# Four conditional layers on one core: first loads in another order, both sines of a rotation together, and the last three queries copied out and normed later

## The chip, the cores and the metric

The kernel runs on 1 core of one Trainium2 chip. Times are device microseconds of that core. TensorE (PE) multiplies, VectorE (DVE), ScalarE (ACT) and GpSimd (POOL) work on elements, SyncE (SP) issues most DMAs; ACT and POOL issue some too.

## The reference

64 sequences of 64 tokens with 512 features pass four residual layers; small integer tables choose per sequence which weights are used.

```python
x = x + (einsum('bsi,bio->bso', x, W0[id]) + b0[id][:, None, :])          # L0, 16 experts
x = x + (einsum('btd,od->bto', x, W1) + s[a] * (x @ A[a].T) @ Bm[a].T)    # L1, 8 adapters of rank 16
# L2: paged attention, 8 query and 4 key heads of 64, window 256, pos = kv_len + 0..63
q, k, v = x @ Wq.T, x @ Wk.T, x @ Wv.T
q, k = rope(rms(q, q_norm_scale), pos), rope(rms(k, k_norm_scale), pos)
# k, v are written into the paged blocks, then attention over the last 256 positions
x = x + softmax(mask(q @ k_all.T / 16)) @ v_all @ Wo.T
x = x + (einsum('bct,bcd->bdt', x, W3[subject]) + bias[subject][:, :, None])   # L3
```

Here `rms(x, g)` is `x * rsqrt(mean(x*x) + 1e-6) * (1 + g)`, and `rope` turns each half-pair by the angle `pos * inv`, with its sine and cosine. All is float32.

## The kernel before

The 4096 tokens are 32 tiles of 128 rows (two sequences each). Every engine runs its instructions in the order in which the program writes them (`manual_schedule`), and so do the queues: the order of the calls is the schedule.

**Phase one** (to about 520 us) goes through the tiles in groups of 1, 1, 2 and then 4. `layer0(i)` multiplies a tile by its two experts' matrices, which `load_w0` fetched (2 x 1 MB a tile, buffers for two tiles); ACT copies the product out as s0; `add_bias` (POOL) makes x plus the bias; `turn0` transposes s0 on PE and DVE adds the two. `layer1(tiles)` multiplies a group by w1 (to whose diagonal blocks the identity is added, for the residual) and by the adapters: pxa, xa, then bo on top. `turn_x2` transposes the result; `keep_kv` makes, norms and rotates the keys and stores them with the values; `parts_q` does that for the queries of earlier tiles and `turn_q` transposes a finished query and stores it to qTd.

`turned` is the common norm and rotation: ACT squares, DVE reduces, ACT takes the square root, then after a `yield` DVE's reciprocal and product, after another `yield` two half products with the sine, one with the cosine (DVE) and an add (engine `X`). `rotation(o)` makes sine and cosine for eight tiles in DVE steps separated by `yield`s, each ending with a Sin on ACT; `other(i)` advances it, `windows` (the row indices of the attention window) and the copies of old cache rows between two matmul groups.

**First loads.** SP loads the tokens' tables (tok1), x of tile 0, W0 of tile 0 in four pieces for one expert (ACT's queue takes the other's), w1, two adapters, x and W0 of tile 1, and so on. Ahead of its W0 pieces ACT's queue issues idcol, toki (all tables to 128 partitions), invf and gain. The bias rows are gathered by POOL (brow), transposed on PE behind the first `layer0` and copied to biasT by ACT (L673).

**The passage.** `gains` for the last seven tiles are made ahead. POOL gathers the keys and values of attention tiles 0 and 1 (`load_kv`), PE makes the queries of tiles 25 to 30 (`product`, L140), which go through `parts_q` on DVE, with `turn_q` (L174) two tiles behind. Then `keys(0)` transposes keys (L823, L829).

**Phase two**: step s of 32 issues `load_kv(s+2)` on POOL and the mask loads on SP, then `scores(s)` (PE L842; DVE adds the mask and takes the maximum, L850; ACT takes the exponential, L854), `attend(s-1)` (L889), `normalise(s)` (DVE), on even steps `last(s-4)` (L929, ACT L936), `project(s-2)` (L917, into the one bank of the pool `pyp`), `keys(s+1)` and `turn(s)` (transposes L875 and L879, copied out by DVE and ACT, L876 and L880). Everything else on PSUM shares a ring of seven banks. The query of tile 31 is made in step 0, in the bank of `pyp`; those of 30 and 31 are rotated and turned in steps 1 to 5:

```python
        else:
            parts[NT - 1] = parts_q(NT - 1, product(NT - 1, wq, "pq", pyp), V, cs[NT - 1])
            turn_q(NT - 3, bp)
        if s == 2:
            next(parts[NT - 1])
        normalise(s, 0)
```

Of the kernel before, what the change touches and what calls it, by code (L numbers as in the profile page):

```python
# [59 lines left out]
def body(ctx: ExitStack, tc: tile.TileContext, a: dict, out: bass.AP):  # L60
# [54 lines left out]

    def turned(ps, n, to, pool, X, kind, cg, sg):

        psv = ps[:, : n * HD].rearrange("p (h d) -> p h d", d=HD)
        sq = pool.tile([128, n, HD], F32, name=f"sq{kind}", bufs=2)
        S.activation(sq, psv, AF.Square)  # L120
        ss = pool.tile([128, n], F32, name=f"ss{kind}", bufs=2)
        V.tensor_reduce(ss, sq, AX.X, ALU.add)
        S.activation(ss, ss, AF.Sqrt, bias=epst, scale=1.0 / HD)
        yield
        rs = pool.tile([128, n], F32, name=f"rs{kind}")
        V.reciprocal(rs, ss)
        qn = pool.tile([128, n, HD], F32, name=f"qn{kind}", bufs=2)
        V.tensor_tensor(qn, psv, bc(rs[:, :, None], [128, n, HD]), ALU.mult)  # L128
        yield
        t2 = sq  # L130
        for f in range(2):
            fs, of = slice(f * HALF, (f + 1) * HALF), slice((1 - f) * HALF, (2 - f) * HALF)
            V.tensor_tensor(t2[:, :, fs], qn[:, :, of], bc(sg[:, None, fs], [128, n, HALF]), ALU.mult)
        V.tensor_tensor(qn, qn, bc(cg[:, None, :], [128, n, HD]), ALU.mult)  # L134
        X.tensor_tensor(to, qn, t2, ALU.add)  # L135
# [6 lines left out]

    def parts_q(i, pq, X, cs=None):
        qr = late.tile([128, H, HD], F32, name="qr", bufs=2)
        qrs[i] = qr.rearrange("p h d -> p (h d)")
        return turned(pq, H, qr, late, X, 0, *(cs or gains(0, i, late, X)))

# [22 lines left out]
    def turn_q(i, pool=late):  # L170
        qrf = qrs.pop(i)
        pqt = bank("pqt")
        for c in range(KC):
            TE.transpose(pqt[:, c * 128 : (c + 1) * 128], qrf[:, c * 128 : (c + 1) * 128], ident)  # L174
        qT = pool.tile([128, 2, 2, 2, T], F32, name="qTs", bufs=2 if pool is late else 4)
        for gp in range(2):
            S.copy(
                qT[:, gp].rearrange("p b h t -> p h b t"),
                pqt[:, gp * 256 : (gp + 1) * 256].rearrange("p (h b t) -> p h b t", h=2, b=2),
            )  # L180
        nc.sync.dma_start(
            qTd[i * 128 : (i + 1) * 128, :], qT.rearrange("p g b h t -> p (g b h t)")
        )

    with ExitStack() as pa:
# [12 lines left out]
        nc.sync.dma_start(tok1.rearrange("p k b -> p (k b)"), a["toks"])  # L198
        idcol = su.tile([B, 1], I32, name="idcol")
        nc.scalar.dma_start(idcol, a["toks"][:, 0:B].rearrange("o b -> b o"))  # L200
        toki = su.tile([128, 4, B], I32, name="toki")
        nc.scalar.dma_start(toki.rearrange("p k b -> p (k b)"), a["toks"].partition_broadcast(128))
        invf = su.tile([128, HALF], F32, name="invf")
        nc.scalar.dma_start(invf, a["invf"].partition_broadcast(128))
        nc.scalar.dma_start(
            gain.rearrange("p k h f -> p (k h f)"), a["gains"].partition_broadcast(128)
        )
        make_identity(nc, ident)
        pidx = su.tile([128, 1], I32, name="pidx")
        P.iota(pidx, pattern=[[0, 1]], base=0, channel_multiplier=1)  # L210
        brow = su.tile([B, D], F32, name="brow", tag="valp")
        P.indirect_dma_start(
            out=brow, out_offset=None, in_=a["b0"],
            in_offset=bass.IndirectOffsetOnAxis(ap=idcol[:, 0:1], axis=0),
        )

# [7 lines left out]
        def load_w0(i, parts=1, queues=(nc.sync, nc.sync)):  # L224

            w0s[i] = []
            for b, queue in zip((2 * i, 2 * i + 1), queues):
                w = wp.tile([128, KC, D], F32, name="w")
                r = queue.value_load(tok1[0:1, 0, b : b + 1], min_val=0, max_val=E - 1)
                for n in range(parts):  # L230
                    cs = slice(n * KC // parts, (n + 1) * KC // parts)
                    queue.dma_start(
                        w[:, cs], a["W0"][bass.ds(r, 1)].rearrange("a (c p) o -> p (a c) o", p=128)[:, cs]
                    )
                w0s[i].append(w)

# [5 lines left out]

        def layer0(i, bias=True):

# [7 lines left out]
            S.copy(s0, p0)  # L252
            if bias:
                add_bias(i)

# [53 lines left out]

        load_x(0)  # L310
        load_w0(0, KC, (nc.sync, nc.scalar))
        load_weight(w1, "w1T")
        load_a(0, range(2))
        load_x(1)
        load_w0(1)
        load_a(0, range(2, 4))
        load_weight(wkv, "wkvT")
        kvi = su.tile([128, 1], I32, name="kvi")
        tabi = su.tile([128, NBLK], I32, name="tabi")
        for h in range(2):  # L320
            hs = slice(h * B, (h + 1) * B)
            nc.scalar.dma_start(kvi[hs], a["toks"][:, 3 * B :].rearrange("o b -> b o"))
            nc.scalar.dma_start(tabi[hs], a["tab"])


        pidxf = su.tile([128, 1], F32, name="pidxf")
        V.tensor_copy(pidxf, pidx)
        p64 = su.tile([128, 1], I32, name="p64")
# [20 lines left out]
        adf = su.tile([128, 8, 8], F32, name="adf")  # L349
        V.tensor_copy(adf.rearrange("p o q -> p (o q)"), toki[:, 1, :])  # L350
        V.tensor_tensor(adf, adf, bc(mine[:, None, :], [128, 8, 8]), ALU.mult)
        ado = su.tile([128, 8], F32, name="ado")
# [12 lines left out]
        def rotation(o):  # L365
# [14 lines left out]
            for name, turn, shift in (("sin", 0.0, 0.0), ("cos", 0.25, 0.5 * PI)):  # L380
# [15 lines left out]
                yield  # L396
                S.activation(r, r, AF.Sin)

        def scalars():

            V.tensor_scalar(gain, gain, 1.0, None, ALU.add)
            V.tensor_scalar(gain[:, 0], gain[:, 0], SCALE, None, ALU.mult)
            V.tensor_scalar(gsw[:, :, 0, :], gain[:, :, 1, :], -1.0, None, ALU.mult)
            V.tensor_copy(gsw[:, :, 1, :], gain[:, :, 0, :])
            V.memset(epst, EPS)
            V.tensor_tensor(eye2, ident[:, :64], ident[:, 64:], ALU.add)
            scale_b(0)


        io = su.tile([128, NBLK], F32, name="io")  # L410
# [201 lines left out]
        def layer1(tiles):  # L612

            o = tiles[0] // 4
            ps = slice(32 * (tiles[0] % 4), 32 * (tiles[-1] % 4) + 32)
            pxa = bank("pxa")
# [47 lines left out]


        scalars()

        biasT = su.tile([128, KC, B], F32, name="biasT")
        layer0(0, False)
        pb = bank("pb")  # L670
        for c in range(KC):
            TE.transpose(pb[:, c * B : (c + 1) * B], brow[:, c * 128 : (c + 1) * 128], ident[:B, :B])
        S.copy(biasT.rearrange("p c b -> p (c b)"), pb[:, : KC * B])  # L673
        add_bias(0)
        turn0(0)
# [4 lines left out]
        for c in range(KC):  # L680
            cs = slice(c * 128, (c + 1) * 128)
            V.tensor_tensor(w1[:, c, cs], w1[:, c, cs], ident, ALU.add)

# [13 lines left out]
        def other(i):  # L697

            next(bg, None)
            next(bg, None)  # L700

            o = (i + 2) // 8
            if 0 < o < NT // 8 and i <= 8 * o + 2:
                next(turns.setdefault(o, rotation(o)), None)
# [4 lines left out]
        for g in range(NG - 1):  # L709
            layer1(tiles[g])  # L710
            if g == 0:
                run(rotation(0))
            elif g == 1:
                far()
            n, m = len(tiles[g]), len(tiles[g + 1])
            for k in range(m):
# [10 lines left out]
                if q is not None:  # L727
                    pq = product(q, wq, "pq")
                turn0(i0)
                if q is not None:  # L730
                    run(parts_q(q, pq, P))
# [228 lines left out]
    load_mask(0)  # L960

    parts = {}
    for i in range(NT - LATE + 1, NT - 1):
        pq = product(i, wq, "pq")
        parts[i] = parts_q(i, pq, V, cs[i])
        next(parts[i])
        if i > NT - LATE + 2:
            turn_q(i - 2, bp)
        if i - 1 in parts:
            run(parts.pop(i - 1))  # L970
        next(parts[i])
    keys(0)
    load_q(1)
    load_mask(1)
    wo = bp.tile([128, KC, D], F32, name="wo", bufs=1)
    for s in range(NT):
        if s + 2 < NT:
            if s < 2:
                after_keys(s)
            load_kv(s + 2)  # L980
            load_mask(s + 2)
        if s and s + 2 < NT:
# [4 lines left out]
        if s:  # L987
            load_pair(s - 1)
            attend(s - 1)
        else:  # L990

            parts[NT - 1] = parts_q(NT - 1, product(NT - 1, wq, "pq", pyp), V, cs[NT - 1])
            turn_q(NT - 3, bp)
        if s == 2:
            next(parts[NT - 1])
        normalise(s, 0)
# [5 lines left out]
        if s + 1 < NT:  # L1002
            keys(s + 1)
        if s in (4, 5):
            turn_q(NT - 6 + s, bp)
        elif s in (2, 3):

            run(parts.pop(NT - 4 + s))
        turn(s)
        if s == 0:  # L1010
            load_q(2)
            nc.sync.dma_start(wo, a["woT"].rearrange("(c p) f -> p c f", p=128))
        elif s == 1:
            next(parts[NT - 1])
    i = NT - 1
# [62 lines left out]
```

## Time and profile before

| | |
|---|---|
| median of 3 runs | 974.5 us (973.77 to 974.64) |
| the profiled execution | 969.85 us |
| its span | 967.9 us |
| mean granted PE clock | 0.995 |
| HBM read, written | 190.29 MB, 69.50 MB |

The profile shows one execution. An engine is busy from the start of an instruction to its end; the ends of matmuls are modelled. A line such as `A <- B: 8.3, 1, 8.3` in a list of waits says that A stood idle until B, 8.3 us in all, once, 8.3 us at most. A bracket behind an instruction in the timeline holds the idle time of the engine before it and what ended it; the two numbers in front are its start and duration. The granted clock is the share of PE's full clock.

### The profile page before, as it was taken

What the parts mean: (1) busy time and instruction counts of PE and PEld (TensorE: products, weight loads), DVE (VectorE), ACT (ScalarE), POOL (GpSimd) and SP (SyncE); (2) the same over time, 40 slices, a digit from 0 to 9 for tenths busy, and PEclk for the clock granted to TensorE, in tenths of its full rate; (3) what the DMA queues carried; (4) which work ended last, traced back from release to release, by engine and by line L of the source; (5) the groups of instructions that cost most, each with busy time, mean ns of one, the idle gap of its engine ahead of it and who ended that gap; (6) DMA issues with size and microseconds to landing.
All of it is one profiled execution on the core that took longest, in us unless ns stands there. A gap on an engine that the chain in (4) does not pass through costs nothing.

```text
span 967.9 us, 17784 instructions
## 1 busy us (share of the span) xinstructions
PE 930.5 (96%) x5397; PEld 506.6 (52%) x5397; DVE 608.7 (63%) x1736; ACT 412.9 (43%) x1084; POOL 404.8 (42%) x599
## 2 busy tenths in 40 slices
PE   5999999999999999999999979999999999999998
PEld 2443443444444444444444556766666666666665
DVE  3756898878573362552226858666667776667673
ACT  0212133232341322422223666656666666666663
POOL 3344265555453454444425543344444333334400
PEclk9999999999999999999999989999999999999999
DMA  7998999999999999999953774766665566566621
GB/s 251 342 324 304 376 375 324 377 393 320 396 330 383 392 339 389 387 351 389 372 218 125 235 261 135 217 214 205 204 194 185 181 194 197 191 204 202 197 69 45
DMA packets 133344, 260.97 MB, mean 270 GB/s; under 512 B 32737, under 2 KB 41570, under 8 KB 133250
## 3 DMA queue, kind: packets, MB, share of 16 engines
q1 hardware_dynamic: 108562, 178.61, 51.6%
q0 software_dynamic: 23280, 79.84, 24.8%
q10 hardware_dynamic: 1408, 1.39, 0.5%
q8 instruction: 43, 0.70, 0.3%
q14 instruction: 51, 0.42, 0.1%
HBM read 190.29 MB, written 69.50 MB: 268 GB/s over the span
## 4 chain that ended last, share of the span: by engine, by line
PE 73%; DVE 2%; ACT 1%; issue 1%; POOL 0%; ACTq 0%
PE py L917 12%; PE po L889 8%; PE ps L842 8%; PE p L635 7%; PE pk L140 7%; PE pq L140 7%; PE p L249 6%; PE ppt L875 6%; PE pkt L823 2%; PE ppt L879 2%; PE pkt L829 1%; PE pz L929 1%; PE pqt L174 1%; DVE pT L876 1%; PE pt L273 1%; PE px L654 1%
## 5 line engine op out<-in xcount | busy, mean ns | idle before, releaser
L769 POOL DMA_INDIRECT kv<-kvd,idxn x128 | 126.6, 989 | 211.1 <-PE po L889 166.9
L854 ACT ACTIVATE pr<-pr,mx 128x320 f32<-128x320 f32 x256 | 140.1, 550 | 7.0 <-DVE mx L850 2.9
L249 PE MATMUL p<-w,xt 128*64 128x512 f32 x512 | 122.2, 606 | 8.5 <-DMA w<-in_W 8.3
L917 PE MATMUL py<-wo,oT 128*128 128x512 f32 (+1 forms) x264 | 118.3, 592 | 1.7 <-DVE qn L128 1.7
L140 PE MATMUL pk<-wkv,x 128*128 128x512 f32 x256 | 115.4, 595 | 2.1 <-ACT x L656 2.1
L155 POOL DMA_INDIRECT st<-in_kvc,cidx x68 | 69.8, 1027 | 107.4 <-DMA kvd<-st 94.3
L635 PE MATMUL p<-w,x 128*128 128x512 f32 x256 | 113.6, 601 | 0.0
L140 PE MATMUL pq<-wq,x 128*128 128x512 f32 x248 | 111.3, 593 | 0.0
L850 DVE CUSTOM_DVE_ANT_0 pr<-ps,mb 128x320 f32<-128x320 f32 x256 | 107.8, 486 | 5.5 <-PE ps L842 2.9
L842 PE MATMUL ps<-kT,qT 64*128 64x320 f32 x512 | 86.9, 459 | 10.9 <-DVE pT L876 6.3
L876 DVE COPY pT<-ppt 128x512 f32<-128x512 f32 x64 | 41.9, 687 | 73.7 <-PE ppt L879 34.5
L866 DVE TENSOR_SCALAR pr<-pr,sm 128x320 f32<-128x320 f32 x256 | 85.4, 395 | 2.2
L889 PE MATMUL po<-pT,kv 128*64 128x128 f32 (+1 forms) x1536 | 84.1, 280 | 1.5 <-issue 1.5
L274 DVE TENSOR_TENSOR x<-pt,x 128x512 f32<-128x512 f32 x32 | 22.0, 688 | 100.6 <-PE pt L273 88.4
L889 PEld LDWEIGHTS po<-pT,kv 128*64 128x64 f32 (+1 forms) x1536 | 70.5, 137 | 22.1 <-DVE mx L850 13.6
L917 PEld LDWEIGHTS py<-wo,oT 128*128 128x128 f32 x264 | 47.5, 189 | 61.5 <-issue 58.4
L635 PEld LDWEIGHTS p<-w,x 128*128 128x128 f32 x256 | 48.3, 192 | 59.0 <-issue 56.7
L249 PEld LDWEIGHTS p<-w,xt 128*64 128x64 f32 x512 | 35.9, 138 | 78.3 <-issue 72.3
L135 POOL TENSOR_TENSOR qr<-qn,sq 128x512 f32<-128x512 f32 x25 | 31.7, 1267 | 105.5 <-DVE qn L134 105.5
L140 PEld LDWEIGHTS pk<-wkv,x 128*128 128x128 f32 x256 | 46.3, 190 | 50.4 <-issue 47.3
L140 PEld LDWEIGHTS pq<-wq,x 128*128 128x128 f32 x248 | 44.9, 190 | 46.2 <-issue 46.2
L842 PEld LDWEIGHTS ps<-kT,qT 64*128 64x128 f32 x512 | 45.2, 187 | 41.4 <-DVE pT L876 20.8
(191 smaller groups left out, 1317.9 us busy)
## 6 DMA issues: line engine op xcount, KB each, us to landing
w<-in_W SPq DMA_DIRECT2D x62, 1024.0 KB
kvd<-st SPq DMA_DIRECT2D x68, 512.0 KB
xt<-in_xT SPq DMA_DIRECT2D x32, 256.0 KB
x2d<-x2n SPq DMA_DIRECT2D x32, 256.0 KB
kvd<-kvn SPq DMA_DIRECT2D x32, 256.0 KB
qTd<-qTs SPq DMA_DIRECT2D x32, 256.0 KB
qT<-qTd SPq DMA_DIRECT2D x32, 256.0 KB
x2r<-x2d SPq DMA_DIRECT2D x32, 256.0 KB
```

What stands on the lines that cost most here:

```text
L140: TE.matmul(ps, x2s[i][:, c, :], w[:, c, :], start=c == 0, stop=c == KC - 1)
L155: P.indirect_dma_start(out=st, out_offset=None, in_=a["kvc"].rearrange("(n r) d -> n (r d)", r=2), in_offset=bass.IndirectOffsetOnAxis(ap= ...
L249: TE.matmul(p0[hs, :], xs[i][:, c, hs], w0s[i][h][:, c, :], start=c == 0, stop=c == KC - 1)
L635: TE.matmul(p1[i], x1s[i][:, c, :], w1[:, c, :], start=c == 0, stop=False)
L769: P.indirect_dma_start(out=kv[:, n, :], out_offset=None, in_=kvd, in_offset=bass.IndirectOffsetOnAxis(ap=at, axis=0),)
L842: TE.matmul(ps[g2][:, :NPOS], qT[rows, gp, b2].rearrange("p h t -> p (h t)"), kT[rows, gp, b2 * NPOS : (b2 + 1) * NPOS], start=True, stop= ...
L850: V.tensor_tensor_reduce(out=p, in0=ps[g2][:, :NPOS], in1=mb[:, b2, :], scale=-1.0, scalar=3.0e38, op0=ALU.add, op1=ALU.min, accum_out=mx[ ...
L854: S.activation(p, p, AF.Exp, bias=mx[:, g, b2 : b2 + 1], scale=-1.0, accum_out=sm[:, g, b2 : b2 + 1],)
L866: V.tensor_scalar(p, p, sm[:, g, b2 : b2 + 1], None, ALU.mult)
L875: TE.transpose(pt[:, n * 128 : (n + 1) * 128], pr[:, g, at : at + 128], ident)
L889: TE.matmul(po[b2][g2 * 64 : (g2 + 1) * 64, gp * 128 : (gp + 1) * 128], kv[rows, n, (G + g) * HD : (G + g + 1) * HD], pT[rows, c, m * 128 ...
L917: TE.matmul(py[:, fs], oT[:, c].rearrange("p b t -> p (b t)"), wo[:, c, fs], start=c == 0, stop=c == KC - 1,)
```

## The change

Four things are changed; nothing is left out of the computation.

1. **First loads.** Gone are idcol, toki and the gather of brow. In their place PE spreads the tables: a product of ones with tok1 (ptok) puts all tables on 128 partitions, and the bias is a product of the whole bias table (btab, loaded first on ACT's queue) with a 0/1 matrix (takes), so that biasT is there before `layer0(0)`. invf and gain go behind the W0 pieces on ACT's queue, the first two adapters ahead of w1 on SP's, the block table (tabi) from ACT's queue to SP's. The register that picks the expert is read once for a piecewise load. The four operations on gain go from DVE to POOL and behind layer1 of tile 0, half of the four w1 adds to POOL, two steps of `windows` behind `turn0(1)`.
2. **Both sines together.** `rotation` does its DVE steps first, then both Sin, then one Sqrt on a spare value. For rotations 1 to 3 this last part runs at the start of `layer1` of tiles 8, 16 and 24.
3. **The passage.** Only tiles 25 to 28 go through `parts_q` there; tile 28's rotation is on POOL (new argument `M`). `keys(0)` comes before the product of tile 29. The products of tiles 29, 30 and 31 (in the passage, step 0 and step 1) are copied to SBUF by ACT (`keep_raw`).
4. **Norm in the steps.** POOL squares them in steps 2 to 4, DVE reduces in steps 3 to 5, one Sqrt for all three in step 6 (followed by an Exp on a spare value), POOL rotates in steps 7 to 9 and `turn_q` follows in steps 8 to 10.

The diff, cut to its core:

```diff
+        btab = su.tile([E, D], F32, name="btab")
+        nc.scalar.dma_start(btab, a["b0"])
...
+        TE.matmul(ptok[:, : 4 * B], one, tokf.rearrange("p k b -> p (k b)"), start=True, stop=True)
...
+        toki = ptok[:, : 4 * B].rearrange("p (k b) -> p k b", k=4)
...
+        V.tensor_scalar(takes, toki[:E, 0, :], pidxf[:E], None, ALU.is_equal)
...
+        for c in range(KC):
+            TE.matmul(pb[:, c * B : (c + 1) * B], btab[:, c * 128 : (c + 1) * 128], takes, start=True, stop=True)
+        V.tensor_copy(biasT.rearrange("p c b -> p (c b)"), pb[:, : KC * B])
...
         load_w0(0, KC, (nc.sync, nc.scalar))
+        load_a(0, range(2))
+        invf = su.tile([128, HALF], F32, name="invf")
+        nc.scalar.dma_start(invf, a["invf"].partition_broadcast(128))
+        nc.scalar.dma_start(gain.rearrange("p k h f -> p (k h f)"), a["gains"].partition_broadcast(128))
         load_weight(w1, "w1T")
-        load_a(0, range(2))
...
         for h in range(2):
-            hs = slice(h * B, (h + 1) * B)
-            nc.scalar.dma_start(kvi[hs], a["toks"][:, 3 * B :].rearrange("o b -> b o"))
-            nc.scalar.dma_start(tabi[hs], a["tab"])
+            nc.sync.dma_start(tabi[h * B : (h + 1) * B], a["tab"])
...
-                S.activation(r, r, AF.Sin)
+            for name in ("sin", "cos"):
+                S.activation(trig[name, o], trig[name, o], AF.Sin)
+
+            S.activation(nul, epst, AF.Sqrt)
...
             o = tiles[0] // 4
+            if tiles[0] and tiles[0] % 8 == 0:
+                run(turns[tiles[0] // 8])
...
-            V.tensor_tensor(w1[:, c, cs], w1[:, c, cs], ident, ALU.add)
+            (P if c % 2 else V).tensor_tensor(w1[:, c, cs], w1[:, c, cs], ident, ALU.add)
+        scale_b(0)
...
+    LAST = NT - 3
...
+    def keep_raw(i, pq):
+        S.copy(raw[:, i - LAST].rearrange("p h d -> p (h d)"), pq)
+
+    def rotate_raw(i):
+        x, t2, (cg, sg) = raw[:, i - LAST], sqr[:, (i - LAST) % 2], cs[i]
+        P.tensor_tensor(x, x, bc(ssr[:, i - LAST, :, None], [128, H, HD]), ALU.mult)
+        for f in range(2):
+            fs, of = slice(f * HALF, (f + 1) * HALF), slice((1 - f) * HALF, (2 - f) * HALF)
+            P.tensor_tensor(t2[:, :, fs], x[:, :, of], bc(sg[:, None, fs], [128, H, HALF]), ALU.mult)
+        P.tensor_tensor(x, x, bc(cg[:, None, :], [128, H, HD]), ALU.mult)
+        P.tensor_tensor(x, x, t2, ALU.add)
+        qrs[i] = x.rearrange("p h d -> p (h d)")
...
-    for i in range(NT - LATE + 1, NT - 1):
-        pq = product(i, wq, "pq")
-        parts[i] = parts_q(i, pq, V, cs[i])
+    for i in range(NT - LATE + 1, LAST):
+        X = P if i == LAST - 1 else V
+        parts[i] = parts_q(i, product(i, wq, "pq"), X, cs[i], X)
...
+    run(parts.pop(LAST - 1))
     keys(0)
+    keep_raw(LAST, product(LAST, wq, "pq"))
+    turn_q(LAST - 2, bp)
...
             load_kv(s + 2)
+            if 2 <= s <= 4:
+
+                x = raw[:, s - 2]
+                P.tensor_tensor(sqr[:, s % 2], x, x, ALU.mult)
+            elif 7 <= s <= 9:
+                rotate_raw(LAST + s - 7)
...
-        else:
-
-            parts[NT - 1] = parts_q(NT - 1, product(NT - 1, wq, "pq", pyp), V, cs[NT - 1])
-            turn_q(NT - 3, bp)
-        if s == 2:
-            next(parts[NT - 1])
+        if s < 2:
+
+            keep_raw(LAST + 1 + s, product(LAST + 1 + s, wq, "pq", pyp))
+            if s == 0:
+                turn_q(LAST - 1, bp)
+        elif s == 6:
+            S.activation(ssr, ssr, AF.Sqrt, bias=epst, scale=1.0 / HD)
+
+            S.activation(ssr1, ssr[:, 0, :1], AF.Exp, scale=-1.0)
+            V.reciprocal(ssr, ssr)
...
-        if s in (4, 5):
-            turn_q(NT - 6 + s, bp)
-        elif s in (2, 3):
-
-            run(parts.pop(NT - 4 + s))
+        if 8 <= s <= 10:
+            turn_q(LAST + s - 8, bp)
+        elif 3 <= s <= 5:
+
+            V.tensor_reduce(ssr[:, s - 3], sqr[:, (s - 3) % 2], AX.X, ALU.add)
```

## The prediction

> **What bounds the kernel now.** First the page: TensorE carries the span, and almost all of what can be won is its idle time and its clock.
>
> ```profile
> span 967.9 us, 17784 instructions
> PE 930.5 (96%) x5397; PEld 506.6 (52%) x5397; DVE 608.7 (63%) x1736; ACT 412.9 (43%) x1084; POOL 404.8 (42%) x599
> ```
>
> The reader is to see 967.9 - 930.5 = 37.4 us of PE idle; no other engine is above 63%. Then the busy times by stretch, to see where the idle lies:
>
> ```profile
> 0.00:8.30 8.30, 0.00 (x0) 0.02 (x1) 2.74 (x18) 0.00 (x0) 2.28 (x10) 1.00 0.43 143
> 8.30:26.70 18.40, 16.06 (x42) 5.98 (x42) 9.09 (x28) 2.14 (x3) 5.89 (x16) 0.91 0.95 317
> 541.30:585.70 44.40, 37.49 (x268) 25.57 (x266) 31.61 (x103) 29.43 (x79) 20.48 (x24) 0.92 0.74 241
> 597.70:648.90 51.20, 50.05 (x429) 34.55 (x428) 35.07 (x123) 32.88 (x96) 20.48 (x23) 1.00 0.64 192
> ```
>
> Columns: stretch, length, busy PE, PEld, DVE, ACT, POOL, granted clock, DMA share, GB/s. The opening has no PE work for 8.3 us and a clock of 0.91 after it; the passage into the attention steps idles 6.9 us of 44.4 at a clock of 0.92, where the steps behind it idle 1.15 of 51.2. Third, the SyncE queue's own waits (0 to 60 us), since the opening waits for W0:
>
> ```profile
> SPq L232 <- DMA w<-in_w1T: 2.1, 1, 2.1
> SPq L232 <- DMA toki<-in_toks: 1.5, 1, 1.5
> SPq L232 <- DMA invf<-in_invf: 1.3, 1, 1.3
> ```
>
> L232 issues W0, and it uses neither toki nor invf: an issue here waits for an older, unrelated load to land. Last, the chain of waits through the passage:
>
> ```profile
> 542.62 1.16 issue
> ...
> 559.11 1.11 issue
> ...
> 566.70 2.27 PE ps L842 x4
> ...
> 569.62 3.55 PE ps L842 x8
> 573.17 3.95 PE po L889 x48
> ...
> 578.04 0.70 DVE qn L128
> ```
>
> Before it scores(0) waits for ACT's copies of kT; at 566.70 four matmuls stand for 2.27 us; the eight and 48 behind them take 3.55 and 3.95 us, against 2.50 for 48 L889 matmuls in the chain further on (granted clock 0.50 from 569.3 to 576.1); at 578.04 project(0) waits until DVE has read tile 31's query out of the one py bank.
>
> **Part 1, the opening.** Removed in front of W0 on ScalarE's queue: four issues (idcol, toki, invf, gain; 0.44 to 0.60 us each); added: btab, one such issue. In before the eight W0 pieces were issued between 3.04 and 7.88 us; the weight loads of L249 show them arriving at 8.28, 10.11, 11.68, 12.38, 12.97, 14.40 and 15.06. In after nothing stands in front but tok1, btab and x(0), so eight issues of 0.34 to 0.39 on two queues end by about 5 us, and data flow from then. Two bounds for the last piece: 2 MB at 317 GB/s (the stretch above) from 5.0 is 11.6; with the old spacing and only ScalarE's 0.86 us (3.90 to 3.04) won it is 14.2. I take 12, nearer the first, because the waits of 1.5 and 1.3 us have no cause left. Behind it, before: copy L252 16.17 to 16.75, transposes 16.81, POOL's bias add L260 only 17.11 to 18.58 (it waited for biasT), DVE add L274 18.62, pxa 19.36. In after biasT is a product with btab at about 5 us and the bias add is done by about 12, so the 1.1 us from 17.5 to 18.62 go too. The PE idle of 1.9 us before pxa was followed by 3.4 us at a clock of 0.50; with 0.8 us of idle left that half-clock spell (1.7 us) probably goes.
>
> W0 of tile 1 is next late: it was issued at 18.26, after the 2.1 us wait for w1 (DMA moved only 102 GB/s from 18 to 20), and 2 MB at the 317 to 380 GB/s of the stretches around it land at about 26, where layer0(1) began at 26.70. So tile 1 wins only what this load wins. In after load_a goes ahead of w1, toki and the gather of brow (0.25 MB, 0.7 us) are gone, and the w1 wait falls away if the earlier W0 pieces free the issue in time: between 1 us (bytes alone) and 6 us (no wait and the stream 3 us earlier). Then xa(1) binds: DVE's rotation and windows work (12 us from 21.27 to 33.7) moves by no more than PE does. **I take -4.8, bounds -1 to -6.5.** Scalars() now runs on POOL after layer1(0) (four short operations, 0.2 to 0.8 us each on DVE, in POOL's idle of 7.74 us before L110: nothing; 2 us if that cover is gone), two of four w1 adds go to POOL beside DVE's two (0.45 us each; L682 took 1.57 in all). tabi moves to SyncE's queue behind wkv: 2 x 0.60 us of issue, read at 30.95, hidden; if not, W0 of tile 2 starts 1.2 us later, inside the 15 us before it is used. The new small PE products fall into PE's first 8.3 idle us.
>
> **Part 2, both sines together.** Each of rotations 1 to 3 paid two loads of the Sin table and two back to Sqrt, 1.28 us each, in the middle of tiles. One pair shows on PE:
>
> ```profile
> 151.51 1.28 ACT L397 ACT_TABLE_LOAD   x1
> 153.12 0.57 ACT L656 COPY x<-px 128x512 f32<-128x512 f32 x1
> 153.74 3.70 PE L140 MATMUL pk<-wkv,x 128*128 128x512 f32 x8 [1.54 <-ACT x L656]
> ```
>
> In after the sines stand at the start of layer1 of tiles 8, 16, 24, where ACT next has x2n to copy after 13.4 us of PE work: hidden. The DVE halves stay in place. **-1.5** (0 if other work delays L656 anyway). The Sqrt load that follows at once also leaves tile 0's first key norm (L123 at 36.08).
>
> **Part 3, the passage.** PE work is equal, so count it at undisturbed rates from 541.3 to 585.7: keys 1.3 + step 0 (2.4 + 3.6 + 0.5 + 1.2 + 2.2) + step 1 (2.4 + 2.5 + 1.2 + 2.2) + step 2 (11.8, the distance 585.69 to 597.45) = 31.3 us against 44.4: **13.1 us are lost there**: 6.9 idle, 3.4 by half clock, the rest inside matmuls that stand. After: product(29) (3.6 us) lies between keys(0) and scores(0) and covers the kT copies (1.2 to 2.0 won); tile 30's five DVE passes (0.75 + 4 x 0.69) no longer precede the first scores; step 1, the shortest (8.3 us of PE against some 7.6 us of scores, exponentials and norms before turn(1)), gets product(31), 3.6 us, so that the 2.1 us wait at 567.5 and the half clock behind it (3.4) have cover; the py bank is freed by an ACT copy (0.58) in step 1, so the 1.68 wait of L917 goes. What stays is the "issue" idle (1.5) that no queue explains, and the like. **I take -9.0, bounds -4 to -13.**
>
> Added, and where it hides: on POOL tile 28's rotation, 2 x 0.72 + 2 x 1.27 = 4.0 us (L135 rows), behind the gathers that end at 538.2, so at 542.2, wanted by turn_q(28) about 545: hidden by 3 us; load_kv(2) is queued behind it and is wanted 15 us later. Squares 3 x 1.27 in steps 2 to 4. rotate_raw 1.27 x 3 + 2 x 0.72 = 5.3 us in steps 7 to 9: with gathers 6.3 and add_one 0.34 POOL needs 12.0 of a 12.4 us step. It waits 6 to 7 us a step for attend anyway, and its gathers are some 24 us ahead of keys, so PE sees nothing; without that cover 5.3 us a step. POOL beside DVE stretched DVE's L470 from 0.43 to 0.50 us (43.4 to 46.7): 23 us of POOL work cost DVE 0 to 3.7 us, mostly in its 33% idle: 0.3. turn_q in steps 8 to 10 in place of 0, 4, 5: same PE (0.6) and ACT (0.65), the SyncE store (0.33) behind load_q: nothing.
>
> Step 6 is the one new wait: Sqrt behind the exponentials, then Exp's table back: 2 x 1.28 + 0.30 + 0.2 = 3.1 us on ACT, ahead of last(2)'s res and the kT copies. ACT idled 4.14 us there in before (631.05 to 635.18). DVE's reciprocal stands before normalise(6) and waits for the Sqrt, so normalise ends some 2.2 us later, with 1.75 us of slack before turn(6): **+0.3, bounds 0 to +5.5** (a 2.1 us wait plus a half-clock spell, as at 567.5). The trace's table load is 1283 ns and the next operation starts 10 ns behind it. [...]
>
> On the clock the trace shows 1.00 for the first matmuls at 8.31, after 8.3 us without any, and 0.50 from 19.9 to 23.3 behind thin work. [...]
>
> **Sum:** -4.8 - 1.5 - 9.0 + 0.6 = -14.7, taken as -14.5. The profiled execution took 969.85 (span 967.9), so 955.4; the median of the runs shown is 4.65 higher, so 974.5 - 14.5 = 960.0.
>
> **Rivals.** A, the gains are half hidden: W0 of tile 1 and the lanes behind it hold PE (opening -1), and the stalls between 558 and 570 have nothing to do with PE's lack of work (DMA share 1.0 to 1.1 there, loads of wo and kv as before), so they come back with their half clock (passage -4): -1 - 1.5 - 4 + 0.6 = -5.9, 968.6. For it: the waits "issue" and the common restart of DVE and ACT at 568.9; against: step 1 gets 3.6 us of work. B, slower: PE waits in its own queue for POOL's rotation at turn_q in steps 8, 9 and 10. A 2.1 us wait with its half-clock spell costs 5.5; three of them and step 6 make 22, less 14.5 is +7.5: 982. It decides from a rotate_raw of about 15 us in place of 5.3, almost three times its rows; the longest L135 row is 1.65 us where 0.72 is usual, so only one tile might be late. C, the opening alone works, because the passage is bound by something else entirely: -4.8 - 1.5 + 0.6 = -5.7, the same place as A.
>
> **Numbers.** Forecast 0.68, A and C 0.20, B 0.07, 0.05 for sums that cancel (0.04 of it within the bound). A run is told from no change at about 0.2%, 2 us. Faster 0.88, same 0.04, slower 0.08. The forecast's own span is -19 to -9; reaching down to A the range is 955.0 to 969.0.
>
> **What would show it.** Right: the first W0 arrival near 6.5 us and the last before 13, layer0(1) before 23; no wait of L232 for toki; one Sin load per rotation; no half-clock spell near 570; the py wait gone; from keys(0) to scores(3), which then holds two more products (7.2 us), 39 to 44 us. Wrong: a half-clock spell anywhere in steps 0 to 10, PE waits at turn_q, or W0 of tile 1 landing at 25 as before.

## The result and the profile after

The changed kernel is slower: 982.34 us (median of four) against 974.57 us of before, ratio 1.0069 with a 95% interval of 1.0045 to 1.0093. The forecast was 960.0. The profiled execution took 981.56 us.

The page of after, to be read against the first fence of the prediction:

```profile
span 979.8 us, 17788 instructions
...
PE 936.4 (96%) x5407; PEld 509.2 (52%) x5407; DVE 602.3 (61%) x1713; ACT 404.2 (41%) x1080; POOL 427.7 (44%) x626
```

Idle time of PE is 979.8 - 936.4 = 43.4 us, 6 more than before, and PE's busy time grew by 5.9 us although the matrix work is the same but for ten small products of the opening: matmuls took longer, part of them at half clock (granted clock 0.50 for 13.7 us in all, in before 10.2). Busy times by stretch of after (columns as in the prediction; the first two rows are the opening, the third runs from 1.5 us before keys(0) to scores(3) and now holds three products where before's holds one):

```profile
0.00:6.56 6.56, 3.48 (x15) 2.59 (x15) 1.13 (x5) 0.00 (x0) 0.86 (x8) 1.00 0.53 175
6.56:24.46 17.90, 13.41 (x39) 4.79 (x39) 9.49 (x36) 1.87 (x2) 9.62 (x22) 0.90 0.93 317
535.80:586.50 50.70, 43.73 (x291) 28.75 (x289) 28.90 (x97) 27.15 (x78) 30.13 (x34) 0.93 0.77 243
```

The reader is to see that layer0(0) starts 1.75 us earlier and layer0(1) at 24.46 instead of 26.70, but that the clock of the opening is still 0.90; and that the passage idles 7.0 of 50.7 us at 0.93, in before 6.9 of 44.4 at 0.92. The SyncE queue's waits of after, 0 to 60 us:

```profile
SPq L297 <- DMA w<-in_W: 3.2, 1, 3.2
SPq L249 <- DMA w<-in_W: 2.9, 3, 1.5
```

L249 issues W0 and no longer waits for toki or invf; but L297, which issues w1, now waits 3.2 us until an older piece of W0 lands. What PE waits for in after, over the whole span:

```profile
PE ps L860 <- DVE pT L894: 12.4, 13, 3.6
PE pt L289 <- ACT s L269: 6.9, 8, 1.9
...
PE p L266 <- DMA w<-in_W: 3.3, 4, 1.7
PE ppt L893 <- DVE pr L884: 2.5, 4, 1.0
PE ps L860 <- issue: 2.4, 1, 2.4
...
PE p L655 <- DVE w L694: 1.8, 1, 1.8
```

The wait of py for tile 31's query (1.7) is gone as forecast. The fourth line is new: PE waits for the normalised probabilities, in step 6 alone. So is the last: PE waits 1.8 us for w1, whose load came late. Set side by side, the starts of after minus those of before are -2.2 us at layer0(1), +0.4 at layer0(29), +1.9 at layer0(31), -1.1 at scores(0), +7.9 at scores(2), +0.8 at scores(3), +1.3 at scores(6), **+7.0 at scores(7)**, +10.1 at scores(13), +11.9 at scores(31). Of the 11.9 us some 4 are probably no effect of the change: the profiled execution of before lay 4.7 us under its median, that of after 0.8.

### The profile page after: what moved, and what is told of

It is laid out like the page before. It is cut to its first block, busy times and chain, and to the rows that moved or that the text cites. A ratio compares the mean times of both kernels' runs of the same rounds, so it can differ in the third digit from the quotient of the medians.

```text
span 979.8 us, 17788 instructions
## 1 busy us (share of the span) xinstructions
PE 936.4 (96%) x5407; PEld 509.2 (52%) x5407; DVE 602.3 (61%) x1713; ACT 404.2 (41%) x1080; POOL 427.7 (44%) x626
## 4 chain that ended last, share of the span: by engine, by line
PE 68%; DVE 3%; ACT 2%; DMA 2%; another core or an unknown queue 1%; issue 1%; SPq 0%; ACTq 0%; POOL 0%
PE py L935 11%; PE po L907 8%; PE ps L860 8%; PE p L655 7%; PE pk L140 7%; PE pq L140 6%; PE p L266 5%; PE ppt L893 5%; PE ppt L897 2%; PE pkt L841 2%; DMA w<-in_W 1%; PE pkt L847 1%; PE pz L947 1%; PE pqt L174 1%; DVE pT L894 1%; ACT pr L872 1%
## 5 line engine op out<-in xcount | busy, mean ns | idle before, releaser
L787 POOL DMA_INDIRECT kv<-kvd,idxn x128 | 126.5, 989 | 204.9 <-PE po L907 150.5
L140 PE MATMUL pk<-wkv,x 128*128 128x512 f32 x256 | 115.6, 596 | 0.6 <-ACT x L676 0.6
L140 PE MATMUL pq<-wq,x 128*128 128x512 f32 x240 | 107.7, 593 | 0.0
L860 PE MATMUL ps<-kT,qT 64*128 64x320 f32 x512 | 90.3, 469 | 15.0 <-DVE pT L894 12.4
L884 DVE TENSOR_SCALAR pr<-pr,sm 128x320 f32<-128x320 f32 x256 | 89.8, 412 | 2.2
L907 PE MATMUL po<-pT,kv 128*64 128x128 f32 (+1 forms) x1536 | 82.1, 278 | 0.0
L907 PEld LDWEIGHTS po<-pT,kv 128*64 128x64 f32 (+1 forms) x1536 | 68.9, 135 | 19.9 <-DVE mx L868 13.7
L123 ACT ACTIVATE ss<-ss,epst 128x4 f32<-128x4 f32 (+1 forms) x61 | 18.2, 299 | 144.2 <-DVE ss L122 131.8
L133 DVE TENSOR_TENSOR sq<-qn,sg 128x128 f32<-128x128 f32 (+1 forms) x120 | 37.1, 350 | 61.2 <-POOL sg L110 59.3
L860 PEld LDWEIGHTS ps<-kT,qT 64*128 64x128 f32 x512 | 47.2, 190 | 47.3 <-DVE pT L894 30.6
```

The source lines that it names most:

```text
L140: TE.matmul(ps, x2s[i][:, c, :], w[:, c, :], start=c == 0, stop=c == KC - 1)
L787: P.indirect_dma_start(out=kv[:, n, :], out_offset=None, in_=kvd, in_offset=bass.IndirectOffsetOnAxis(ap=at, axis=0),)
L860: TE.matmul(ps[g2][:, :NPOS], qT[rows, gp, b2].rearrange("p h t -> p (h t)"), kT[rows, gp, b2 * NPOS : (b2 + 1) * NPOS], start=True, stop= ...
L884: V.tensor_scalar(p, p, sm[:, g, b2 : b2 + 1], None, ALU.mult)
L907: TE.matmul(po[b2][g2 * 64 : (g2 + 1) * 64, gp * 128 : (gp + 1) * 128], kv[rows, n, (G + g) * HD : (G + g + 1) * HD], pT[rows, c, m * 128 ...
```

## Experiments

Theory at the start: three losses, each in its own place: the opening's lead is not kept through the layers; the stall of the passage was never one of missing PE work; and step 6 makes DVE late. Rivals for step 6: ACT's table loads by themselves, the wait of DVE for the Sqrt, or POOL's rotation beside DVE.

### The parts by themselves (four runs on one chip; before 972.68 us there)

**Opening and sines only.** Before with the new opening and rotations; the passage and steps untouched.

> The kernel before with the new opening and both sines together; the passage and the steps as before. By the prediction's terms (-4.8 and -1.5) 968.3 us. By the theory that the trace of after suggests, the start of layer0(1) is 2.2 us earlier but the gain is given back before the last tiles of layer 1 (there the trace of after stands +0.2 to +0.7 us, tile 31 +3.7): 974 to 976 us, so no change.

Measured 972.54 us, ratio 0.9997 (0.9983 to 1.0011). So the 6.3 us that the prediction counted there do not exist in the end time, although layer0(1) started 4.4 us earlier in this profile than in before's.

**Passage only.** Before with `keep_raw`, `rotate_raw` and the norm in the steps; opening and rotations untouched.

> The kernel before with the last three queries copied out and normed in the steps; the opening and the rotations as before. By the prediction's terms (-9.0 and +0.6) 966.2 us. By the theory from the trace of after (the passage wins about 2 us, step 6 loses 5.7, the rotations of steps 7 to 10 lose 3, the steps behind them 1.8) about +8.5: 983 us.

Measured 979.49 us, ratio 1.0062 (1.0037 to 1.0086). Nearly the whole loss is in this half. In its profile step 6 takes 19.3 us, in before 13.6.

**The reciprocal behind normalise.** The third run:

```
         elif s == 6:
             S.activation(ssr, ssr, AF.Sqrt, ...)
             S.activation(ssr1, ssr[:, 0, :1], AF.Exp, scale=-1.0)
-            V.reciprocal(ssr, ssr)
         normalise(s, 0)
         normalise(s, 1)
+        if s == 6:
+            V.reciprocal(ssr, ssr)
```

> The changed kernel with one line moved: in step 6 DVE's reciprocal of the nine roots stands behind normalise(6), no longer ahead of it; so POOL's rotation, which waits for it, starts behind normalise too. If the 5.7 us lost in step 6 are the wait of DVE for ACT's Sqrt and the start of POOL beside normalise, they go: 977 us, and PE waits no more for pr in step 6. If ACT's two table loads themselves hold PE (kT copies late), 981 or more remains.

Measured 969.62 us, ratio 0.9973 (0.9955 to 0.9991): one line moved turns the change from a loss into a small gain. Step 6 takes 13.58 us, before's 13.64. ACT's two table loads stay in their place there (a block of 3.1 us in after), so they cost nothing by themselves.

**The rotations on DVE.** `rotate_raw` issues its five operations on DVE in place of POOL; the reciprocal stays ahead of normalise, as in the change.

> The changed kernel with the five multiplications of each of the three late rotations on DVE in place of POOL, in the same program place (start of steps 7 to 9). If POOL's work beside DVE is what stretches normalise (four multiplies in 2.96 and 4.12 us in place of 1.3), step 6 gives 3 to 4 us back, and steps 7 to 9 pay DVE 3.4 us each, most of it in its idle third: 978 us. If the wait for the Sqrt is all, step 6 stays at +5.7 and steps 7 to 9 get worse: 984 us.

Measured 984.77 us, ratio 1.0129 (1.0104 to 1.0154). The number is that of the rival (984), but the steps speak against it: step 6 takes 14.75 us and does not stay at its loss of 5.7. So without POOL's work DVE's wait for the Sqrt costs 1.1 us; the other 4.6 of the change's loss in step 6 need POOL. The loss lies elsewhere: the rotations ahead of the scores' passes on DVE cost 3.8 to 4.9 us in each of steps 7, 8 and 9, more than the 3.4 expected, so POOL was the better engine for them.

Step 6 in DVE's timeline (start, duration, engine, line, operation, number of them, idle before). First before, the two halves of normalise:

```profile
629.74 1.40 DVE L866 TENSOR_SCALAR pr<-pr,sm 128x320 f32<-128x320 f32 x4
...
631.26 1.27 DVE L866 TENSOR_SCALAR pr<-pr,sm 128x320 f32<-128x320 f32 x4
```

Then after:

```profile
635.04 0.30 DVE L1046 RECIPROCAL ssr<-ssr 128x24 f32<-128x24 f32 x1 [3.45 <-ACT ssr L1045]
...
635.41 2.96 DVE L884 TENSOR_SCALAR pr<-pr,sm 128x320 f32<-128x320 f32 x4
...
638.49 4.12 DVE L884 TENSOR_SCALAR pr<-pr,sm 128x320 f32<-128x320 f32 x4
```

and POOL's timeline of after:

```profile
636.15 0.95 POOL L787 DMA_INDIRECT kv<-kvd,idxh  x1 [0.30 <-issue]
637.13 1.05 POOL L992 TENSOR_TENSOR raw<-raw,ssr 128x512 f32<-128x512 f32 x1
638.25 1.49 POOL L995 TENSOR_TENSOR sqr<-raw,sg 128x256 f32<-128x256 f32 x2
639.82 1.26 POOL L996 TENSOR_TENSOR raw<-raw,cg 128x512 f32<-128x512 f32 x1
641.17 1.26 POOL L997 TENSOR_TENSOR raw<-raw,sqr 128x512 f32<-128x512 f32 x1
```

DVE's timeline of the third run, the same multiplications, the reciprocal, and one of the scores' passes that follow:

```profile
626.96 1.40 DVE L884 TENSOR_SCALAR pr<-pr,sm 128x320 f32<-128x320 f32 x4
...
628.48 1.27 DVE L884 TENSOR_SCALAR pr<-pr,sm 128x320 f32<-128x320 f32 x4
630.30 0.30 DVE L1049 RECIPROCAL ssr<-ssr 128x24 f32<-128x24 f32 x1 [0.55 <-ACT ssr L1045]
...
635.37 0.49 DVE L868 CUSTOM_DVE_ANT_0 pr<-ps,mb 128x320 f32<-128x320 f32 x1
```

and the start of POOL's rotation there:

```profile
631.53 0.94 POOL L787 DMA_INDIRECT kv<-kvd,idxh  x1 [0.30 <-issue]
632.49 1.06 POOL L992 TENSOR_TENSOR raw<-raw,ssr 128x512 f32<-128x512 f32 x1
```

POOL's queue is about a step ahead of PE, so the rotation that the program writes into step 7 falls into the time of step 6. In both kernels it starts right behind the last gather (L787), 12.3 us behind the first matmul of scores(6), when the reciprocal has been done for 1.8 and 1.9 us. So the reciprocal's place does not decide when POOL starts, as the expectation of the third run had it; it decides when DVE normalises: 10.6 us behind that matmul in after, 6.8 in the third run. In after DVE's wait of 3.45 us pushes normalise into the time of the rotation. From 637 to 642 POOL's multiplications and DVE's L884 then run beside each other, and eight L884, 3.17 us together in before, take 7.55; the longest single one takes 1.87 instead of 0.37 to 0.52. Each of the last five L884 ends 0.18 or 0.19 us behind the end of one of POOL's five operations, and POOL's operations take about as long as in the third run: DVE waits for POOL, one operation at a time. In the third run POOL rotates from 632.49 to 637.76, beside DVE's passes over the scores, and those keep their 0.48 to 0.49 us. So it is this operation of DVE that POOL holds up, not DVE as such. One thing that sets the two apart in the kernel: L884 multiplies probabilities by a column, with its large input and its output in SBUF (up to 1.87 us beside POOL), while one input of the scores' pass is the product in PSUM (0.49 us beside POOL). Whether that is the cause was not shown. By the records the first L884 that was held began at 636.50, ahead of POOL's multiplication at 637.13, and still ended behind it, at 638.37 against 638.18.

### The stall of the passage (four runs on a second chip; before 972.29 us there)

All four edit the third run's kernel.

**wo early.** `wo` is allocated and loaded behind `load_mask(0)`, ahead of the late products of the passage.

> The kernel of the third run (changed kernel, reciprocal behind normalise), with the load of wo (1 MB) issued before the six late products in place of the end of step 0. The stall of all engines in step 1 (10 us between the starts of scores(1) and scores(2) beyond before's distance) begins while ten gathers of kv, six mask loads and wo are on the DMA queues. If the load on the queues makes it, 1 MB less of it shortens the stall: 963 to 967 us. If not (the stall comes with the place in the program, whatever is loaded), 969.6 us as before the edit.

Measured 967.11 us, ratio 0.9949 (0.9932 to 0.9967).

**wo late.** The load of `wo` stands at the end of step 1.

> The same kernel with the load of wo issued at the end of step 1 in place of step 0; project(0), its first reader, comes in step 2. By the theory of the load on the queues the stall of step 1 shortens, but may come back in step 2: 965 to 970 us. By the rival 969.6 us, the stall unchanged in place and length.

Measured 971.64 us, ratio 0.9996 (0.9981 to 1.0011).

**kv(3) later.**

```
-            load_kv(s + 2)
+            if s != 1:
+                load_kv(s + 2)
 ...
             attend(s - 1)
+            if s == 1:
+                P.tensor_copy(bp.tile([1, 1], F32, name="seen"), oTs[0][0:1, 0, 0, 0:1])
+                load_kv(3)
```

> The same kernel as the third run, with the five gathers of kv(3) issued behind attend(0) (POOL waits for oT(0)) in place of the start of step 1, where they follow the five of kv(2) without a break. By the theory of the load on the queues this takes 1.3 MB out of the stretch where all engines stand: the stall and its half-clock spell go, 960 to 964 us. By the rival 969.6 us.

Measured 972.29 us, ratio 0.9998 (0.9980 to 1.0016).

In none of the three does the stall go; it moves. (The stall: 10 us of the third run in which PE is busy for 4.5 us, DVE for 1.7 and ACT for 1.8.) PE's busy time in its worst 10 us of the passage, and where that lies: third run 4.5 us (545 to 555), wo early 5.9 (530 to 540), wo late 5.0 (550 to 560), kv(3) later 3.6 (560 to 570). Wo early is the best of them, but against the third run, measured on the other chip, the intervals overlap. The other two, which also take load out of step 1, are no better than the third run, so the theory of the load alone is not borne out.

**Sines of rotation(0) behind the copies.**

```
-                run(rotation(0))
+                first = rotation(0)
+                for _ in range(4):
+                    next(first)
 ...
                     turn_x2(i)
+                if g == 0:
+                    run(first)
```

> The same kernel as the third run, with rotation(0)'s two sines and the small Sqrt on ACT behind the copies of s(1) and x2(0) in place of ahead of them; the DVE work of the rotation stays. If ACT's two table loads ahead of the copy of s(1) are what gives the opening's gain back between layer0(1) and layer0(2) (PE waits 1.7 to 2.0 us at L289), this wins 1.5 to 2 us: 967.9 us, tile 2 some 4 us earlier than in before in place of 2.2. If another wait takes its place (key norm of tile 0 for the later tables), 969.6 us.

Measured 969.88 us, ratio 0.9980 (0.9965 to 0.9994), no better than the third run. PE's wait for s(1) fell (L289 in the first 47 us from 3.3 to 1.8 us in all), but in this profile w1 came late and PE waited 2.2 us for its added identity instead of 0.3, so that layer0(1) began at 24.8 us instead of 21.8. Inconclusive for ACT's part; it shows that another wait stands ready in the opening.

### A chip without the stall (four runs; before 950.88 us there)

**Sines only.** Before with both sines at the start of layer 1 and the small Sqrt behind them.

> The kernel before with both sines of a rotation together at the start of layer 1 and the small Sqrt behind them; opening, passage and steps as before. By the prediction's term (-1.5) 970.8 us at a time before of 972.3; if ACT's shorter work in the middle of the tiles frees nothing that PE or the DMA queues wait for, 972.3, and then the 0.3 us that opening and sines won together are all there is in either.

Measured 950.42 us, ratio 0.9992 (0.9981 to 1.0003). PE's wait pk from x (L140) fell from 2.1 to 0.6 us, exactly the forecast 1.5, but its wait pxa from x rose from 3.8 to 4.7 and one for W0 of 0.5 is new (against the one profile of before, from another chip).

**No gathers for tiles 2 and 3.**

```
     def load_kv(i):
+        if i in (2, 3):
+            kvs[i] = kvs[i - 2]
+            return
```

> The third run's kernel without the ten gathers of kv(2) and kv(3): steps 2 and 3 use the keys and values of tiles 0 and 1 (so the output rows of tiles 2 and 3 are other ones). 2.6 of some 10 MB that the queues move between 530 and 570 us are gone. If the load on the queues makes the stall of all engines in the passage, it goes, with its half-clock spell: 961 to 963 us, scores(3) some 8 us earlier. If the stall comes with the first steps whatever is loaded, 969.6 us.

Measured 943.82 us, ratio 0.9920 (0.9901 to 0.9939).

**No rotation.** `rotate_raw` only names the raw query.

> The third run's kernel with POOL's three rotations left out (tiles 29 to 31 use the raw queries, so their rows are other ones); squares, roots and reciprocals stay. If POOL's 15 us of rotations in steps 6 to 9 delay DVE or the gathers, as the 1.4 us lost in steps 7 to 13 suggest, 968.2 us; if those 1.4 us are the three turn_q there, 969.6 us.

Measured 944.72 us, ratio 0.9935 (0.9915 to 0.9956).

**wo in layer 1.** `wo` uses w1's buffer, loaded behind `layer1(tiles[-1])`.

> The third run's kernel with wo loaded into w1's buffer right behind the last layer 1, some 40 us earlier than the end of step 0, where the queues are less busy (143 to 217 GB/s in the page's slices around 500 us, 350 and more in the layers). If the load on the queues in the passage makes the stall, 1 MB less of it, moved to where nothing waits, saves what 1 MB takes at 350 GB/s, 3 us, or more with the half-clock spell: 963 to 967 us. If not, 969.6 us.

Measured 944.42 us, ratio 0.9935 (0.9914 to 0.9957).

Before itself is 22 us faster on this chip, and no kernel shows the stall here: in the last two PE is busy in all 40 us from 530 to 570. Steps 6 to 9 take 12.61, 11.75, 13.05 and 12.19 us with the rotations and 12.61, 11.75, 13.05 and 12.19 without: POOL's rotations in steps 7 to 9 are free, and the 0.44 us more in steps 8 to 10 is `turn_q`.

What differs between the chips shows in the third run's timeline on the first chip (kinds of engines mixed, in order of time):

```profile
548.78 0.02 SPq L181 DMA_DIRECT2D qTd<-qTs  x1
...
548.83 0.58 ACT L848 COPY kT<-pkt 128x512 f32<-128x512 f32 x1 [3.10 <-remote]
...
551.64 0.00 SPq L808 DMA_DIRECT2D mb<-maskd  x1
551.68 0.69 DVE L894 COPY pT<-ppt 128x512 f32<-128x512 f32 x1 [6.11 <-PE ps L860]
...
554.48 0.01 SPq L810 DMA_DIRECT2D mb<-maskd  x1
554.54 1.07 ACT L894 COPY pT<-ppt 128x512 f32<-128x512 f32 x2 [5.13 <-PE ps L860]
554.60 0.69 DVE L894 COPY pT<-ppt 128x512 f32<-128x512 f32 x1 [2.23 <-PE ps L860]
```

SyncE, ACT and DVE, which wait for different things, go on at the same instants, 2.85 us apart. ACT's L848 waits only for four PE transposes that had begun by 544.10; PE's signal is recorded at 548.81. In the trace's record of semaphore updates, all engines and all loads together, there are 107 gaps of more than 0.62 us between 530 and 930 us here, typically of 0.7 us; before has 103, after 117. On the chip of these four runs there are 0 to 3.

### The change and its mends on one chip (four runs; before 951.44 us there)

The changed kernel, the third run's, the one without gathers for tiles 2 and 3, and the one with wo in layer 1, beside each other.

> The changed kernel, measured beside the next three on one chip. The chips differ: on two of them the traces of steps 0 to 31 hold over 100 gaps of 0.63 us and more without a semaphore update of any engine, 97% of them inside POOL's runs of gathers (shifted by 1 us), on a third none. On a chip with the gaps 1.007 times before, as first measured; on a chip without them the passage gains 6 us and step 6 still loses some 5: 1.000 times before.

> The third run's kernel (reciprocal behind normalise(6)) on the same chip. With the gaps 0.997 times before, without them 0.9935, like the kernel with wo moved on that chip. In both cases 5 to 10 us below the changed kernel.

> The kernel without the gathers of kv(2) and kv(3) on the same chip (steps 2 and 3 use tiles 0 and 1). If the gathers make the stall of all engines, then on a chip with the gaps the stall of 8 to 10 us in the passage goes: 0.990 times before, 7 us below the run before this one; on a chip without them, nothing to win, 0.992 as measured there.

> The kernel with wo loaded behind the last layer 1 on the same chip. If the stall follows the gathers and not wo, on a chip with the gaps 0.996 times before, at most 1 or 2 us below the kernel with only the reciprocal moved; if wo's megabyte lengthens it, 0.993. On a chip without them 0.9935.

Measured, in this order: 950.73 us, ratio 0.9995 (0.9978 to 1.0012); 945.29, 0.9928 (0.9905 to 0.9952); 946.91, 0.9945 (0.9928 to 0.9962); 945.51, 0.9935 (0.9913 to 0.9957). This chip has no gaps either (0 to 2), so the gathers and wo could not be told apart by time. It gives step 6 without any other disturbance: 16.26 us in the change, 12.61 with the reciprocal moved, 3.65 us, and normalise takes 6.33 us there against 3.16.

Busy times of the passage of the third run's kernel, on the first chip:

```profile
545.00:555.00 10.00, 4.52 (x21) 2.40 (x19) 1.65 (x4) 1.77 (x4) 6.00 (x8) 0.82 0.87 268
555.00:565.00 10.00, 9.82 (x64) 7.15 (x65) 6.15 (x25) 5.45 (x19) 1.74 (x2) 0.67 0.89 297
```

and of the same kernel on this one:

```profile
545.00:555.00 10.00, 10.00 (x62) 6.67 (x58) 8.00 (x31) 9.30 (x29) 8.07 (x11) 1.00 0.80 256
555.00:565.00 10.00, 10.00 (x92) 7.36 (x92) 6.97 (x24) 6.84 (x21) 7.56 (x9) 1.00 1.04 380
```

Same instructions, the same share of the DMA engines and more (1.04), no idle PE and no lower clock. So a busy DMA alone does not make the stall.

### Gathers or masks (two runs on a further chip; before 950.87 us there)

The third run's kernel without gathers from tile 2 on, and without mask loads from tile 2 on.

> The kernel with the reciprocal behind normalise, without POOL's gathers from tile 2 on (steps 2 to 31 use the keys and values of tiles 0 and 1; their output rows are other ones). On a chip with the gaps between semaphore updates: if the gathers make the gaps, none is left in steps 2 to 31, steps take 12.6 and 11.75 us by turns in place of 13.5 and 11.8, and the time falls by the stall and 0.9 us in every second step: 0.972 times before. If something else makes them, gaps and steps stay as they are: 0.997. On a chip without gaps 0.993 either way.

> The same kernel with the gathers kept and the three mask loads of each step left out from tile 2 on (steps use the masks of tiles 0 and 1; output rows are other ones). SP was seen held at these issues for 1.4 us while the gaps lasted. On a chip with the gaps: if the mask loads make them, 0.972 times before; if SP is only held like every other engine, the gaps and the even steps of 13.5 us stay and the time is 0.99 to 0.997. On a chip without gaps 0.993.

Measured 947.69 us, ratio 0.9968 (0.9950 to 0.9987), and 943.89, 0.9930 (0.9904 to 0.9955). The chip has no gaps, so what makes them on the others stays open. But the first of the two, expected at 0.993, is slower than the third run's kernel on the chips without gaps, and its profile says why. Without gathers POOL runs ahead, does its three rotations in a row, and meets normalise(7). DVE's timeline:

```profile
632.93 4.14 DVE L887 TENSOR_SCALAR pr<-pr,sm 128x320 f32<-128x320 f32 x4
```

and POOL's:

```profile
632.70 1.50 POOL L998 TENSOR_TENSOR sqr<-raw,sg 128x256 f32<-128x256 f32 x2
634.28 1.26 POOL L999 TENSOR_TENSOR raw<-raw,cg 128x512 f32<-128x512 f32 x1
635.62 1.26 POOL L1000 TENSOR_TENSOR raw<-raw,sqr 128x512 f32<-128x512 f32 x1
```

The eight multiplications take 7.96 us in place of 3.06 and step 7 takes 14.30 us in place of 11.75: the loss of the changed kernel again, 2.6 us of it, in another step, with nothing of ACT or of a reciprocal near it.

## Why the prediction was wrong, point by point

**Step 6 (+0.3, bounds 0 to +5.5) is the step that failed outright.** ACT's block was sized well: forecast 3.1 us, in after 3.1 (631.88 to 635.00), and harmless by itself. The wait of DVE was seen, and costs 1.1 us by itself. What was missed is where it puts normalise: beside POOL's rotation. The price of that stands in the prediction's sentence on POOL: it priced POOL beside DVE by L470, which went from 0.43 to 0.50 us, and gave 0.3 us for the whole change. The operation that POOL met was L866 (L884 in after), which no POOL arithmetic but the short add_one ran beside in before; there the price is 4.4 us in one step. The loss is 3.65 us where nothing else disturbs, and 5.7 us with a half-clock spell behind it on the chips with gaps (in after the granted clock was 0.50 from 642.4 to 645.9 us). Between medians the third run's kernel is 5.4 us below the change on the chip where both ran. On the chips with gaps steps 7 to 11 of after also take 3.0 us longer than before's, those of the third run 1.4; turn_q explains 1.3 of either, the rest is open.

**The passage (-9.0, bounds -4 to -13) had the right work and the wrong cause.** From layer0(31) to scores(3) before takes 113.4 us, after 112.3, the third run 111.6: 1.1 to 1.8 us won. On the chips without gaps the same distance is 106.4 in the sines-only kernel, whose passage is before's, and 100.8 to 101.1 in the change and the third run's kernel: 5.3 to 5.6 us won, in three single profiles. There keys(0) to scores(3) takes 38.3 to 38.9 us (forecast 39 to 44), in after 49.3. So the term is too large even without the stall. Its floor was too low: the 31.3 us counted for before's stretch take 36.7 on a chip without gaps. The step that failed is the reading of the 2.1 us wait at 567.5 and of the half clock behind it as PE's lack of work, which product(31) would cover. Rival A named the sign: DVE and ACT restart together at 568.9. It was put at 0.20, and for the passage it was right.

**The opening (-4.8) and the sines (-1.5): each first step true, neither kept.** The arrival of W0(0), the missing waits for toki and invf, the one Sin load for each rotation are there. Yet layer0(1) starts at 24.5 us in after: w1, issued 3.2 us late, holds PE for 1.8 us, and the half-clock spell that was to go is still there (granted clock 0.50 from 17.8 to 21.2 us). Where PE waited only 0.3 us for w1 (the third run) layer0(1) starts at 21.8. But most of that lead is gone by layer0(2). In the run with the opening and sines alone it is 4.4 us at layer0(1) and 1.8 at layer0(2): layer0(1) itself takes 4.72 us (3.98 in before), PE then waits 1.69 us for ACT's copy of s(1), which now stands behind both sines and their table loads, and 0.4 for xa(1). At layer0(31) that profile still has 1.8 us; in after 2.9 more are lost, with waits for W0 (2.0 us behind 47 us, none in before) among the causes. By the medians' ratio opening and sines together are worth 0.3 us (between 1.1 us lost and 1.7 won, of 972.7). The failed step is that a wait taken from PE was counted as time won: the sum let xa(1) bind next, and had no term for the copy of s(1). The sines behind the copies took that wait away, but w1 was late in its profile, so that this cause alone is responsible is not shown. Nor is what becomes of the 1.8 us behind layer0(31).

**The clock of the first matmuls was misread.** The first record of the granted clock begins at 12.90 us in before and 10.98 in after; the 1.00 ahead of it has no record behind it. In after the first eight matmuls of layer0(0) start in pairs 0.85 to 0.90 us apart, the last eight 0.43 to 0.48: layer0(0) begins at about half speed, where the prediction read 1.00. It does so in before too (by the profile its first seven matmuls take 1.08 us on average, the last seven, behind 13 us, 0.61), so no term of the sum hangs on it.

**POOL's rotations in steps 7 to 9 (hidden) and turn_q (nothing): right, but for 0.44 us in each of three steps.** Rival B put its loss at turn_q in steps 8 to 10; PE waits there for nothing. Its 982 is almost the measured 982.34, by luck: three late rotations were to make it, and they cost nothing; the loss is in step 6, where B counted 5.5 of its 22 us.

The reciprocal moved is faster than both kernels: 0.9973 of before with gaps, 0.9928 without, and with wo early 0.9949 with gaps.

## What to carry to other kernels

Price contention of two engines by the very instruction that will meet the other engine, not by one that happens to run beside it in the old trace (here L470 with 0.43 and 0.50 us, where eight L884 went from 3.17 to 7.55); and where a new wait moves a piece of work, ask what the other engines do at the time to which it moves. The stall in which engines with different waits resumed at the same instants was not cured by more work for PE (the passage idles 7.0 us of 50.7 with three products in it, 6.9 of 44.4 with one). A lead at the start of a stretch is a gain at its end only if all that PE needs further on comes as much earlier: of 4.4 us at layer0(1) 1.8 were left at layer0(2).

## What the hardware did that was not expected

The same program takes 972 to 975 us on some chips and 951 on others. On the first, semaphore updates of all engines come in bursts about 0.7 us apart for stretches of some microseconds (102 to 119 gaps of more than 0.62 us between 530 and 930 us with the gathers kept); 97% and 98% of the gaps of the third run and of before lie in POOL's runs of gathers moved 1 us later, against 48% of the time that these runs fill. On three other chips there are 0 to 3. Every second step takes 13.5 us with them and 12.61 without. That the gathers make them was not shown: the runs without gathers came to chips that have none.
